# Attention's value bias added to the residual stream by GpSimd, row statistics gathered by fours, and the values of two batches by seven products of 129-column blocks

## The chip, the core and the metric

The kernel runs on one core of a Trainium2 chip. The core has a matrix engine (TensorE, PE in the profile; PEld are its weight loads), VectorE (DVE), ScalarE (ACT), GpSimd (POOL) and SyncE (SP, which here issues DMAs only). The metric is the device time of one execution in microseconds (us), as the median of several runs.

## The reference

The input x has 4 batches of 1024 tokens with 256 features, in fp32. Four blocks follow each other, each behind a layer normalization and with a residual:

```python
x = x + attention(layernorm(x))      # causal, one head of 256
x = x + ffn(layernorm(x))            # r * (relu(k)**2 @ Wv), token shift
x = x + state_space(layernorm(x))    # gated, with a long convolution
x = x + ffn(layernorm(x))            # same weights as before

# attention
Q, K, V = X @ Wq.T + bq, X @ Wk.T + bk, X @ Wv.T + bv
weights = softmax(where(causal, -inf, Q @ K.T / 16))
return weights @ V
```

A row of softmax weights sums to one, so `weights @ (X @ Wv.T + bv)` is `weights @ (X @ Wv.T) + bv`.

## The kernel before

**Tiles.** A batch is two halves of 512 tokens, numbered j (0 to 7), and a half is four row tiles of 128 tokens, numbered i over the whole input (0 to 31). The suffixes a, f, h, g of names stand for the four blocks: attention, first ffn, state space, second ffn. All matrix products are fp32, which TensorE does in two passes each; the profile counts the passes.

**Order.** The kernel first logs all its work with an `Order` object. `o.unit` logs a piece of TensorE work and `o.op` a piece of other work, with what it needs, and with one or several ways (an engine and an estimated cost). A planner then chooses the order and, for each op with several ways, the engine that would end first (`_way`, L256), and emits everything in that order. So the queue of each engine is fixed when the program is built, and each engine works its queue in order. Buffers in PSUM are two pairs of banks ("pair") and four single banks ("bank"). A pool of 34 slots of 4 x 257 numbers per partition holds what is as large as half a batch.

**Normalization** (`normalized`, L584). Per row tile VectorE makes `bn_stats` (st, L622) and `bn_aggr` (mv, L623). Then, for all four rows (in the first half, two and two), VectorE adds epsilon (ve, L648), GpSimd raises to the power -1/2 (rs, L661), VectorE makes the shift (mrs, L670), and VectorE (L676) or ScalarE (L682) makes each normalized row (xn). The rows are then turned to features by tokens, by transposes on TensorE (pt, L775 and L1455) or through DRAM.

**Attention.** Scores are taken as x M x^T with M made from both weights, so that only one side ("queries") is projected, and the other is the stream xa itself. `values(i)` (L1512) makes the values of a row tile: two products of 257 columns into a bank (pv, L1522), of which 256 are the value features and the last gives a score bias of the key side; VectorE then adds the bias row `bv_r` to all 257 and writes v (L1532). `scores(i)` (L1536) makes up to 1024 scores (sc, L1550), and VectorE adds the mask to the diagonal block (L1560) and takes the row's minimum with v's last column added (L1566); ScalarE makes the exponents (L1571). `weigh(i)` (L1647) multiplies with the values (po, L1655), and VectorE scales this and adds it to the stream x (L1664).

**Seven products** (`seven_products`, L840). A product of 2 x 2 blocks by seven block products instead of eight, used for the queries of batches 2 and 3 (`queries_of_batch`, from `SEVEN_FROM`), for the gates (zs), skips (ss) of the state block and for keys (gks) of the second ffn. It works on a chain in PSUM: p1, p6, p7, p4 follow each other in one bank, p5 and p3 in another, p2 in a third. Between them copies u1, u2, u3 (L783 on ScalarE, L784 on VectorE) and adds c11, c22, c12 (L905, L907) are made, and c21 is the end of the chain:

```python
unit(6, ..., [f"{key}.u1", f"{sums_key}.T2"], chain, first=False)
kept("u2", 6, 1)
...
unit(7, ..., [f"{key}.u2", f"{sums_key}.T3"], chain, first=False)
kept("u3", 7, 0, [f"{key}.c11"])
```

T1 to T4 are sums of blocks of the stream (`stream_sums`, L815: GpSimd or VectorE, L832); the sums of weight blocks are made once (`weight_sums`, L808).

**Second ffn.** `pr` (L928) are row products: pr_g.pr the gate, pr_g.pv the values, which need ka_g, the squared relu of the keys (ScalarE L1046 and L1047 for one of a chain's quarters). The stages after attention overlap with it and with each other; of the last half, g7, nothing follows but its own work.

Of the kernel before, what the change touches and what calls it, by code (L numbers as in the profile page):

```python
# [19 lines left out]
P = 128  # L20
NB = 4
L = 1024
D = 256
# [7 lines left out]
SLOT = 4 * (D + 1)  # L31
# [22 lines left out]
class Order:  # L54
# [17 lines left out]
    SURE = 0.5  # L72
    FRONT = 12.0
# [182 lines left out]
    def _way(self, time, n):  # L256

        if self.log[n]["moves"]:
            time = max(time, self.queue - self.FLIGHT - 0.5)
        return min(  # L260
            (self._start(time, w) + w[1], self._start(time, w), w[0], w[2])
            for w in self.log[n]["ways"]
        )
# [96 lines left out]
def dve(n):  # L360
    return 0.02 + n / 850
# [7 lines left out]
def hybrid_kernel(  # L369
# [41 lines left out]
    slots = ctx.enter_context(tc.tile_pool(name="slots", bufs=34))  # L411
# [92 lines left out]
    wv = new("wv", KC, D + 1)  # L504
    bv_r = new("bv_r", D + 1)
    bq_c, bk_c, dsk, dt_c = (new(n, KC) for n in ("bq_c", "bk_c", "dsk", "dt_c"))
# [14 lines left out]
    load(2.0, "wv", *stream_rows(wv[:, :, :D], WvT), *per_row(bv_r[:, :D], bv))  # L521
# [62 lines left out]
    def normalized(  # L584
# [36 lines left out]
        def stats(n):  # L621
            nc.vector.bn_stats(st()[:, n, :], row(n))  # L622
            nc.vector.bn_aggr(mv()[:, n, :], st()[:, n, :])  # L623
# [69 lines left out]
        if by_scalar:  # L693
            for n in range(NH):
                o.op(f"{key}.su{n}", [needs[n]], ("ACT", act(D) + 0.11, partial(sums, n)))
            o.op(f"{key}.me", [f"{key}.su{n}" for n in range(NH)], ("POOL", 0.2, means))
            for n in range(NH):
                o.op(f"{key}.st{n}", [f"{key}.me"], ("ACT", act(D) + 0.11, partial(squares, n)))
            variances_of = lambda n0, n1: by_sums()
            shifts_of = lambda n0, n1: shifts_by_sums()  # L700
        else:
            for n in range(NH):
                o.op(f"{key}.st{n}", [needs[n]], ("DVE", 0.53, partial(stats, n)))
            variances_of, shifts_of = variances, shifts
        for n0, n1 in spans:
            span = "" if n1 - n0 == NH else f"{n0}"
            some = range(n0, n1)
            o.op(
                f"{key}.ve{span}", [f"{key}.st{n}" for n in some],
                ("DVE+port", 0.08 * k, partial(variances_of, n0, n1)),  # L710
            )
            o.op(
                f"{key}.rs{span}", [f"{key}.ve{span}"],
                ("POOL", 0.4 + 0.62 * k, partial(powers, n0, n1)),
            )
            o.op(
                f"{key}.mrs{span}", [f"{key}.rs{span}"],
                ("DVE+port", 0.08 * k, partial(shifts_of, n0, n1)),
            )
            for n in some:  # L720
                o.op(
                    f"{key}.xn{n}", [f"{key}.mrs{span}"],
                    ("DVE+port", dve(D), partial(on_vector_by_sums if by_scalar else on_vector, n)),
                    ("ACT", act(D) + 0.1, partial(on_scalar, n)),
                )
# [89 lines left out]
    def stream_sums(key, src, needs):  # L815

        t = [lazy(lambda k=k: cols(f"T{k}_{key}")) for k in range(KC)]

        def b(c, h):
            return src(h)[:, c, :]  # L820

        def sums(k):
            return t[(k - 1) // 2]()[:, (k - 1) % 2, :]

        for k, plus, minus in (
            (1, lambda: b(0, 1), lambda: b(0, 0)),
            (3, lambda: b(1, 1), lambda: b(0, 1)),
            (2, lambda: b(1, 1), lambda: sums(1)),
            (4, lambda: b(1, 0), lambda: sums(2)),
        ):  # L830
            def emit(engine, k=k, plus=plus, minus=minus):
                engine.tensor_sub(sums(k), plus(), minus())  # L832

            o.op(
                f"{key}.T{k}", needs + ([f"{key}.T{k - 1}"] if k in (2, 4) else []),
                ("POOL", 1.05, partial(emit, nc.gpsimd)), ("DVE+port", dve(HALF), partial(emit, nc.vector)),
            )
        return sums

    def seven_products(key, sums_key, a, s_of, src, t_of, add_to, direct, needs, there):  # L840


        u = lazy(lambda: slot(f"u_{key}"))
        held = lazy(lambda: pair(f"held_{key}"))

        def part(k):
            return lambda: u()[:, ts(k, HALF)]

        def chain():
            return held()[:, :HALF]  # L850

        def shared():
            return held()[:, HALF:]

        def unit(r, w, data, need, dst, takes=None, first=True):
            o.unit(
                f"{key}.p{r}", columns(HALF), needs + need,
                lambda: nc.tensor.matmul(  # L858
                    dst(), lhsT=w(), rhs=data(), start=first, stop=True, skip_group_check=True
                ),  # L860
                takes,
            )

        def kept(name, r, k, more=()):
            o.op(f"{key}.{name}", [f"{key}.p{r}", *more], *copies(part(k), chain))

        unit(1, lambda: a(0, 0), lambda: src(0)[:, 0, :], there, chain, "pair")
        kept("u1", 1, 0)
        yield
        p = lazy(lambda: bank(f"p2_{key}"))  # L870
        unit(2, lambda: a(0, 1), lambda: src(0)[:, 1, :], there, p, "bank")
        o.op(
            f"{key}.c11", [f"{key}.p2", f"{key}.u1"],
            ("DVE", dve(HALF) + 0.03, partial(add_to, 0, 0, p, part(0))), frees="bank",
        )
        yield
        unit(6, lambda: s_of(2), lambda: t_of(2), [f"{key}.u1", f"{sums_key}.T2"], chain, first=False)
        kept("u2", 6, 1)
        yield
        unit(5, lambda: s_of(1), lambda: t_of(1), [f"{key}.p1", f"{sums_key}.T1"], shared)  # L880
        yield
        unit(7, lambda: s_of(3), lambda: t_of(3), [f"{key}.u2", f"{sums_key}.T3"], chain, first=False)
        kept("u3", 7, 0, [f"{key}.c11"])
        o.op(
            f"{key}.c22", [f"{key}.p5", f"{key}.u3"],
            ("DVE", dve(HALF) + 0.03, partial(add_to, 1, 1, shared, part(0))),
        )
        yield
        unit(4, lambda: a(1, 1), lambda: t_of(4), [f"{key}.u3", f"{sums_key}.T4"], chain, first=False)
        o.op(f"{key}.c21", [f"{key}.p4"], *direct(1, 0, chain))  # L890
        yield
        unit(
            3, lambda: s_of(4), lambda: src(1)[:, 1, :], [f"{key}.c22"] + there, shared, first=False
        )
        o.op(
            f"{key}.c12", [f"{key}.p3", f"{key}.u2"],
            ("DVE", dve(HALF) + 0.03, partial(add_to, 0, 1, shared, part(1))),
        )
        o.op(None, [f"{key}.c21", f"{key}.c12"], ("none", 0.0, lambda: None), frees="pair", lag=0.0)
        yield  # L900
# [45 lines left out]
    class Mix:  # L946
# [74 lines left out]
        def keys_of_batch(self, b):  # L1021
# [29 lines left out]
            for e, h in ((0, 0), (1, 1), (0, 1)):  # L1051
# [7 lines left out]
                key, key, fk_block, lambda k: fk_sums[:, k - 1, :], src, T,  # L1059
# [305 lines left out]
    def score_weights():  # L1365
# [42 lines left out]
        def store_behind():  # L1408
            nc.vector.tensor_scalar_mul(wv[:, :, D : D + 1], pm()[:, :, D : D + 1], -1.0 / 16.0)
# [27 lines left out]
    def attend_prepare(j, by_hand=False):  # L1437
# [6 lines left out]
        )  # L1444

# [44 lines left out]

    def queries_of_batch(b):
# [8 lines left out]
        T = stream_sums(key, src, there)  # L1500
        for name, needs in (
# [6 lines left out]
            key, key, wm_block, lambda k: q_sums[:, k - 1, :], src, T,  # L1508
# [3 lines left out]
    def values(i):  # L1512

        j, n = divmod(i, NH)
        if n == 0:
            v[j] = lazy(lambda: rows(f"v_{j}", D + 1))
# [3 lines left out]
        def emit():  # L1520
            for c in range(KC):
                nc.tensor.matmul(  # L1522
                    pv()[:, : D + 1], lhsT=xaj()[:, c, ts(n, P)], rhs=wv[:, c, :],
# [4 lines left out]
            f"pv{i}", columns(D + 1, 2), [f"a{j}.xa{c}" for c in range(KC)] + ["wvb"], emit, "bank"  # L1528
# [3 lines left out]
            ("DVE", dve(D), lambda: nc.vector.tensor_add(t()[:, n, :], pv()[:, : D + 1], bv_r)),  # L1532
            frees="bank",
        )

    def scores(i):  # L1536
# [21 lines left out]
        def least():  # L1558
# [3 lines left out]
            if i >= TURNED_BY_DRAM:  # L1562
# [4 lines left out]
                dst, src, v[2 * b + h]()[:, n, D : D + 1], None, ALU.add, ALU.min, accum_out=nmx(),  # L1567
# [15 lines left out]
        o.op(f"p{i}", [f"sc{i}", f"v{i}"], ("DVE", dve(nk) + 0.3, least), frees="pair")  # L1583
# [63 lines left out]
    def weigh(i):  # L1647
# [5 lines left out]
        def emit():  # L1653
            for n in range(t + 1):
# [3 lines left out]
                    rhs=v[2 * b + n // NH]()[:, n % NH, :D],  # L1658
# [15 lines left out]
        o.op(f"a.x{i}", [f"po{i}", f"rsm{i}"], ("DVE", dve(D) + 0.05, add), frees="bank")  # L1674
# [63 lines left out]
    def gates_of_batch(b):  # L1738
# [20 lines left out]
        for e, h in ((0, 0), (1, 1), (0, 1)):  # L1759
# [5 lines left out]
            key, key, wz_block, lambda k: z_sums[:, k - 1, :], src, T,  # L1765
# [162 lines left out]
    def skips_of_batch(b):  # L1928
# [3 lines left out]
        for j in (2 * b, 2 * b + 1):  # L1932
# [5 lines left out]
            f"ss{b}", f"zs{b}", wx_block, lambda k: x_sums[:, k - 1, :], src, sums_of_batch(b),  # L1938
# [3 lines left out]
    def mix_states(b):  # L1942
# [25 lines left out]
        for h in range(2):  # L1968
            j = 2 * b + h
            for e in range(KC):  # L1970
# [7 lines left out]
                    ("POOL", 1.05, partial(gated, nc.gpsimd, j, e)),  # L1978
# [74 lines left out]

    scored, valued = -1, 0
    for i in range(-2, NI):
# [18 lines left out]
        if 0 < j < 2 * NB:  # L2074
# [8 lines left out]
            if k == 3 and j % 2 == 1 and SEVEN_FROM <= j // 2 + 1 < NB:  # L2083
                chain = queries_of_batch(j // 2 + 1)
                behind = len(o.log)
        while valued < min(i + (3 if i < AHEAD_FROM else 4), NI - 1):
            valued += 1
            values(valued)
# [176 lines left out]
```

## Time and profile before

| | |
|---|---|
| median of three runs | 465.31 us (464.91 to 465.99) |
| the profiled execution | 464.18 us |
| its span in the profile | 462.4 us |
| TensorE, weight loads busy | 454.6, 311.4 us |
| VectorE, ScalarE, GpSimd busy | 370.7, 227.0, 139.4 us |
| granted TensorE clock | 1.00 |
| values: TensorE passes of 257 columns | 128 |
| values: VectorE adds | 32, 13.2 us |

The span is the time between the first and the last instruction that the profile shows. Busy times add up the instructions of an engine. A mean duration of a matmul is longer than its share of time, because matmuls are pipelined: how fast they follow each other is read from the starts of neighbours. "Idle before" and "waits" name the instruction whose end released an engine.

### The profile page before, as it was taken

Reading aid. Unit: us, or ns where it says so; the run is one execution under the profiler, and the core shown is the slowest. Engines: PE = TensorE matmul, PEld = TensorE weight load, DVE = VectorE, ACT = ScalarE, POOL = GpSimd, SP = SyncE. Lnnn points to the kernel's source line nnn. Section 1 sums busy time; section 2 is a strip of 40 time slices with the busy share of each in tenths; the row PEclk is TensorE's granted clock in tenths of the full one; section 3 lists DMA queues with packets and bytes.
Section 4 is the critical chain, followed back from the end, with each engine's and each line's share of the span. In section 5 each row is a group of like instructions: output and inputs, shape, how many; then the busy total and the mean of one; then the engine's idle time right before and its main releaser. Section 6 shows DMA issues by size and latency. Waiting matters only on the chain.

```text
span 462.4 us, 6630 instructions
## 1 busy us (share of the span) xinstructions
PE 454.6 (98%) x2052; PEld 311.4 (67%) x2052; DVE 370.7 (80%) x914; ACT 227.0 (49%) x473; POOL 139.4 (30%) x145
## 2 busy tenths in 40 slices
PE   8999999999999999999999999999999999999996
PEld 5665776667786767776678774473565857686675
DVE  4898697989989888788989977425689989998852
ACT  3322334453284453554335755523467887743452
POOL 3001002303032412332221568512255216336240
PEclk9999999999999999999999999999999999999999
DMA  8067958684358641428784869503014042604522
GB/s 236 27 170 209 272 143 236 169 252 151 101 160 213 184 138 51 137 87 256 226 261 128 276 220 276 213 15 90 13 63 121 0 143 86 215 14 135 178 75 68
DMA packets 84915, 69.44 MB, mean 150 GB/s; under 512 B 20160, under 2 KB 82576, under 8 KB 84880
## 3 DMA queue, kind: packets, MB, share of 16 engines
q1 hardware_dynamic: 84064, 68.76, 50.2%
q8 instruction: 16, 0.26, 0.2%
q10 hardware_dynamic: 816, 0.26, 0.2%
q14 instruction: 19, 0.16, 0.1%
HBM read 40.54 MB, written 28.45 MB: 149 GB/s over the span
## 4 chain that ended last, share of the span: by engine, by line
PE 84%; DVE 10%; POOL 3%; issue 1%; SPq 1%; DMA 1%; ACT 0%; DVEq 0%; POOLq 0%
PE po L1655 14%; PE sc L1550 13%; PE pv L1522 6%; PE held_zs L858 3%; PE held_ss L858 3%; PE held_qs L858 2%; PE held_gks L858 2%; PE pc L1862 2%; PE dust L1339 1%; DVE T_gks L832 1%; DVE xr_g L977 1%; DVE xk_g L977 1%; POOL x L1101 1%; PE pp_a0.pq L793 1%; PE pp_g6.pk L793 1%
## 5 line engine op out<-in xcount | busy, mean ns | idle before, releaser
L1655 PE MATMUL po<-v,prT 128*128 128x256 f32 x288 | 67.6, 380 | 0.0
L1550 PE MATMUL sc<-xa,q 128*128 128x512 f32 (+3 forms) x192 | 66.9, 486 | 0.0
L1655 PEld LDWEIGHTS po<-v,prT 128*128 128x128 f32 x288 | 54.2, 189 | 11.6 <-issue 3.1
L1571 ACT ACTIVATE pr<-pr,nmx 128x128 f32<-128x128 f32 (+7 forms) x32 | 24.7, 773 | 69.7 <-DVE pr L1566 57.1
L1550 PEld LDWEIGHTS sc<-xa,q 128*128 128x128 f32 x192 | 34.8, 190 | 24.3 <-issue 20.1
L1522 PE MATMUL pv<-wv,xa 128*128 128x257 f32 x128 | 32.7, 380 | 0.0
L1101 POOL TENSOR_TENSOR x<-x,r_f 128x512 f32<-128x512 f32 x16 | 20.8, 1298 | 35.7 <-DVE r_f L1095 33.8
L1522 PEld LDWEIGHTS pv<-wv,xa 128*128 128x128 f32 x128 | 23.9, 191 | 8.4 <-issue 4.1
L1608 DVE STREAM_TRANSPOSE prT<-pblocks 128x384 f32<-128x384 f32 (+7 forms) x30 | 24.0, 798 | 4.8 <-DMA pblocks<-exps 4.8
L661 POOL TENSOR_TENSOR rs_h<-ve_h,minus_half 128x8 f32<-128x8 f32 x8 | 13.2, 1646 | 47.9 <-DVE ve_h L650 47.9
L1566 DVE TENSOR_SCALAR_CACHE_REDUCE pr<-sc,v 128x128 f32<-128x128 f32 (+7 forms) x32 | 26.2, 818 | 1.1
L661 POOL TENSOR_TENSOR rs_a<-ve_a,minus_half 128x4 f32<-128x4 f32 x7 | 7.4, 1060 | 62.8 <-DVE ve_a L648 52.9
L1101 POOL TENSOR_TENSOR x<-x,r_g 128x512 f32<-128x512 f32 x14 | 20.1, 1446 | 16.8 <-DVE r_g L1095 16.8
L1699 POOL TENSOR_TENSOR x<-x,bout_r 128x512 f32<-128x512 f32 x16 | 20.7, 1302 | 13.3 <-ACT x L1692 9.8
L1692 ACT ACTIVATE x<-x,mrs_h,rs 128x256 f32<-128x256 f32 x32 | 17.2, 588 | 6.5 <-DVE rs L1703 6.5
L1965 POOL TENSOR_TENSOR z<-z,skip 128x512 f32<-128x512 f32 x11 | 15.0, 1384 | 17.4 <-DVE skip L1961 17.3
L661 POOL TENSOR_TENSOR rs_f<-ve_f,minus_half 128x4 f32<-128x4 f32 x8 | 8.1, 1016 | 39.2 <-DVE ve_f L648 34.1
L1664 DVE SCALAR_TENSOR_TENSOR x<-po,rsm,x 128x256 f32<-128x256 f32 x32 | 14.9, 467 | 5.4 <-PE po L1655 5.3
L622 DVE BATCH_NORM_STATS2 st_a<-x 128x6 f32<-128x256 f32 x32 | 13.0, 407 | 3.0 <-DMA x<-in_L_attn_a_X_dram 3.0
L974 ACT ACTIVATE xk_g<-hT_g,muk 128x512 f32<-128x512 f32 x16 | 11.0, 713 | 8.4 <-DVE hT_g L750 8.4
L1532 DVE TENSOR_TENSOR v<-pv,bv_r 128x257 f32<-128x257 f32 x32 | 13.2, 413 | 2.2 <-PE pv L1522 1.8
L977 DVE SCALAR_TENSOR_TENSOR xr_g<-hT_g,mur,xr_g 128x512 f32<-128x512 f32 x16 | 14.4, 920 | 0.5 <-ACT xr_g L974 0.5
(478 smaller groups left out, 1070.3 us busy)
## 6 DMA issues: line engine op xcount, KB each, us to landing
hk<-r_dram SPq DMA_DIRECT2D x16, 512.0 KB, 6.6
rows_g<-xn_g SPq DMA_DIRECT2D x8, 512.0 KB, 3.0
blocks_g<-rows_g SPq DMA_DIRECT2D x32, 128.0 KB, 2.7
x<-in_L_attn_a_X_dram SPq DMA_DIRECT2D x7, 512.0 KB, 5.1
rows_f<-xn_f SPq DMA_DIRECT2D x7, 512.0 KB, 3.5
blocks_f<-rows_f SPq DMA_DIRECT2D x28, 128.0 KB, 2.7
rows_h<-xn_h SPq DMA_DIRECT2D x7, 512.0 KB, 3.3
blocks_h<-rows_h SPq DMA_DIRECT2D x28, 128.0 KB, 2.9
```

Of the source, the lines that this page charges most:

```text
L661: nc.gpsimd.tensor_tensor(rs()[:, :k].rearrange("p k n -> p (k n)"), ve()[:, :k].rearrange("p k n -> p (k n)"), minus_half[:, : k * NH], A ...
L858: lambda: nc.tensor.matmul(dst(), lhsT=w(), rhs=data(), start=first, stop=True, skip_group_check=True),
L977: nc.vector.scalar_tensor_tensor(t()[:, c, :], hT()[:, c, :HALF], mu1[:, c : c + 1], t()[:, c, :], ALU.mult, ALU.add,)
L1101: nc.gpsimd.tensor_add(xg, xg, r()[:, ts(g, 2), :])
L1522: nc.tensor.matmul(pv()[:, : D + 1], lhsT=xaj()[:, c, ts(n, P)], rhs=wv[:, c, :], start=(c == 0), stop=(c == KC - 1),)
L1550: nc.tensor.matmul(sc()[:, k * HALF : k * HALF + w], lhsT=qh()[:, c, ts(n, P)], rhs=keys[k]()[:, c, :w], start=(c == 0), stop=(c == KC - 1),)
L1566: nc.vector.tensor_scalar(dst, src, v[2 * b + h]()[:, n, D : D + 1], None, ALU.add, ALU.min, accum_out=nmx(),)
L1571: nc.scalar.activation(p()[:, :nk], p()[:, :nk], AF.Exp, bias=nmx(), scale=-1.0, accum_out=sm())
L1608: nc.vector.transpose(dst()[:, : NH * width].rearrange("p (k m a) -> p k m a", m=NH, a=GRP), blocks().rearrange("p m (k a) -> p k m a", a= ...
L1655: nc.tensor.matmul(po()[:, :D], lhsT=src()[:, ts(n, P)], rhs=v[2 * b + n // NH]()[:, n % NH, :D], start=(n == 0), stop=(n == t),)
L1692: nc.scalar.activation(xt, xt, AF.Identity, bias=mrs()[:, 0, n : n + 1], scale=rs1()[:, n : n + 1])
L1699: nc.gpsimd.tensor_add(xg, xg, bout_r.unsqueeze(1).to_broadcast([P, 2, D]))
```

## The change

1. **Value bias.** `values` no longer adds `bv_r`. The values are copied out of PSUM by ScalarE or VectorE, and GpSimd adds the bias only in the last column (`whole_bias`, one [128 x 1] add per row tile, for which the minimum now waits). GpSimd adds bv to the stream x itself, once per two row tiles, after these rows have been normalized (`shifted`); the add of the attention's output to x waits for it.
2. **Statistics.** The four `bn_aggr` of a half are made together after its `bn_stats`.
3. **Layout.** The value weights get a zero column in front, so that they have 258 columns in two blocks of 129. The values stand in columns 1 to 256.
4. **Values by seven products** for batches 2 and 3, in two groups of row tiles per batch. Each product is two matmuls of 129 columns, one per row tile, with the sums T of the queries' chain as weights and blocks of the value weights (or their sums `v_sums`) as moving data. The chain takes two single banks. The queries' and the values' chains of a batch are logged alternately (`attended`).
5. **Planner.** VectorE gets a handicap of 0.5 us where another engine could do an op (`SPARED`); the estimated cost of two GpSimd ops goes from 1.05 to 1.25; there are 33 slots instead of 34, each a little larger.

```diff
-SLOT = 4 * (D + 1)
+VW = D + 2
+SLOT = 4 * VW
...
+    SPARED = 0.5
...
+        for engine, cost, emit in ways:
+            start = self._start(time, (engine, cost, emit))
+            late = start + cost
+            if len(ways) > 1 and engine[:3] == "DVE":
+                late += self.SPARED
+            if late < best:
+                best, chosen = late, (start + cost, start, engine, emit)
...
-    slots = ctx.enter_context(tc.tile_pool(name="slots", bufs=34))
+    slots = ctx.enter_context(tc.tile_pool(name="slots", bufs=33))
...
+    nc.gpsimd.memset(wv[:, :, 0:1], 0.0)
...
         def stats(n):
             nc.vector.bn_stats(st()[:, n, :], row(n))
-            nc.vector.bn_aggr(mv()[:, n, :], st()[:, n, :])
+
+        def gather(n0, n1):
+            for n in range(n0, n1):
+                nc.vector.bn_aggr(mv()[:, n, :], st()[:, n, :])
...
-                ("POOL", 1.05, partial(emit, nc.gpsimd)), ("DVE+port", dve(HALF), partial(emit, nc.vector)),
+                ("POOL", 1.25, partial(emit, nc.gpsimd)), ("DVE+port", dve(HALF), partial(emit, nc.vector)),
...
+    def row_products(tiles, width, *of):
+
+        def emit(dst, w, data, first):
+            for n, t in enumerate(tiles):
+                nc.tensor.matmul(
+                    dst()[:, ts(n, width)], lhsT=data()[:, ts(t, P)], rhs=w(),
+                    start=first and n == 0, stop=True, skip_group_check=True,
+                )
+
+        return len(tiles) * width, columns(width, len(tiles)), operands(*of), emit
...
+        def shifted(g):
...
+            nc.gpsimd.tensor_add(xg, xg, bv_r[:, :D].unsqueeze(1).to_broadcast([P, 2, D]))
+
+        for g in range(2):
+            o.op(
+                f"a{j}.b{g}", [f"a{j}.xn{2 * g + n}" for n in range(2)] + ["wv"],
+                ("POOL", 1.27, partial(shifted, g)), delay=1.0 + g,
+            )
...
         o.op(
             f"v{i}", [f"pv{i}"],
-            ("DVE", dve(D), lambda: nc.vector.tensor_add(t()[:, n, :], pv()[:, : D + 1], bv_r)),
-            frees="bank",
+            *copies(lambda: t()[:, n, :], lambda: pv()[:, :VW], VW), frees="bank",
         )
+        whole_bias(i)
...
+            ("POOL", 0.15, lambda: nc.gpsimd.tensor_add(
+                t()[:, n, D + 1 :], t()[:, n, D + 1 :], bv_r[:, D:])),
...
+    def values_of_batch(b, T):
...
+        for g in range(2):
+            key = f"vs{b}{g}"
...
+            yield from seven_products(
+                key, f"qs{b}",
+                row_products(
+                    range(2 * g, 2 * g + 2), VW // 2, wv_block, lambda k: v_sums[:, k - 1, :], src, T
+                ),
+                add_to, direct, ["v_sums"], there, kind="bank",
+            )
...
-        o.op(f"p{i}", [f"sc{i}", f"v{i}"], ("DVE", dve(nk) + 0.3, least), frees="pair")
+        o.op(f"p{i}", [f"sc{i}", f"vc{i}"], ("DVE", dve(nk) + 0.3, least), frees="pair")
...
+    def attended(b):
+
+        queries = queries_of_batch(b)
+        next(queries)
+        yield
+        values = values_of_batch(b, query_sums[b])
+        for _ in range(6):
+            next(queries)
+            yield
+            next(values)
+            yield
+        for _ in values:
+            yield
```

## The prediction

> **What bounds the kernel now.** I read the busy line and the slices first, then the stages, the waits of TensorE (PE), the chain, the groups. The page:
>
> ```profile
> PE 454.6 (98%) x2052; PEld 311.4 (67%) x2052; DVE 370.7 (80%) x914; ACT 227.0 (49%) x473; POOL 139.4 (30%) x145
> PE   8999999999999999999999999999999999999996
> DVE  4898697989989888788989977425689989998852
> PEclk9999999999999999999999999999999999999999
> ```
>
> PE is busy throughout at a full granted clock; VectorE (DVE) is second, 90% busy or more in many slices. A busy PE need not be at its pace, so the stages (span from start to end; PE, PEld, DVE, ACT, POOL busy) and PE's waits come next:
>
> ```profile
> 140.00:180.00 40.00, 40.00 (x161) 26.76 (x160) 34.49 (x85) 16.94 (x31) 12.74 (x16) 1.00 0.57 161
> 285.00:300.00 15.00, 14.71 (x70) 6.25 (x69) 7.23 (x15) 8.66 (x16) 8.41 (x8) 1.00 0.69 256
> 336.00:370.00 34.00, 34.00 (x133) 23.73 (x132) 30.97 (x51) 25.06 (x77) 14.85 (x18) 1.00 0.20 63
> 370.00:400.00 30.00, 30.00 (x113) 19.69 (x112) 27.41 (x52) 24.14 (x62) 13.03 (x12) 1.00 0.42 132
> ...
> PE pr_g4.pv L928 <- ACT ka_g L1047: 0.9, 1, 0.9
> PE held_gks L858 <- DVE u_gks L784: 0.9, 1, 0.9
> PE held_zs L858 <- DVE z L907: 0.6, 1, 0.6
> PE pt_h7.T L775 <- DVE xn_h L676: 0.3, 1, 0.3
> ```
>
> In attention (to about 285 us) PE never waits, though DVE is 86 to 90% busy: relieving DVE there buys nothing by itself. PE's waits after the start come to 2.7 us here, 3.3 us by start-to-start times. So the change can gain what it takes from PE's own work, plus some of those 3.3, less what it adds in waits.
>
> PE's pace is read from the chain (start, length, count of passes; an fp32 product is two passes):
>
> ```profile
> 18.38 0.87 PE pv L1522 x4
> 20.86 0.87 PE pt_a1.xa L1455 x8
> ```
>
> A value pass (257 columns) takes 0.87/4 = 0.217 us, a 128-column pass with its own weights 0.87/8 = 0.109. In the timeline two 512-column passes start at 407.63 and the next work at 408.49: 0.43 each. Time is proportional to columns from 512 to 128.
>
> **Part by part.** *Seven products, batches 2 and 3.* Out go 16 row tiles of 4 passes: 64 x 0.217 = 13.9 us. In come 4 groups x 7 products x 2 tiles x 2 passes = 112 passes of 129 columns, at 0.110: 12.3 us. The other 64 passes grow by one column, 0.05 in all. Net **-1.5 us**, all on the path.
>
> [...]
>
> *VectorE's relief.* The rows:
>
> ```profile
> L1532 DVE TENSOR_TENSOR v<-pv,bv_r 128x257 f32<-128x257 f32 x32 | 13.2, 413 | 2.2 <-PE pv L1522 1.8
> L1699 POOL TENSOR_TENSOR x<-x,bout_r 128x512 f32<-128x512 f32 x16 | 20.7, 1302 | 13.3 <-ACT x L1692 9.8
> L783 ACT COPY u_gks<-held_gks 128x512 f32<-128x512 f32 x6 | 3.5, 583 | 3.3 <-PE held_gks L858 3.3
> ```
>
> The order of the changed program gives the counts. DVE loses 32 value adds (-13.2), 27 normalized rows that go to ScalarE (ACT; at 0.41, those of f at 0.56: -12.7), 6 copies u (-4.1), 5 relu steps (-3), and gains 12 chain adds at some 0.42 (+5): 28 less. Gathering the bn_aggr takes little busy time away, but the pair bn_stats and bn_aggr has a pitch of 0.53 now and four bn_aggr can follow each other at about 0.1: some 0.06 a tile, so its queue is shorter by about 6 more. ACT gets 27 x 0.59 + 15 value copies and 16 chain copies at about 0.38 (a 128x256 copy of wq) + 6 x 0.583 + 5 x 0.62 and a few more: +37, to 57% of the span. POOL gets 16 bias adds at 1.30 (20.8), 32 one-column adds at 0.18 (its two-column copies: 5.8), and a net few stream sums: about +32. All of it lies beside PE work in attention: scores run two or three rows ahead of the minimum that now waits for the one-column add. Cost taken: nothing; if that cover failed, each late minimum would cost its POOL queue, about 1.3 us. The bias adds move no DMA; SP's queue keeps its order but for hk loads issued later with some 5 us in hand.
>
> When POOL reads SBUF, DVE pays: a T_gks sum took 1.64 us beside a POOL sum and 0.69 just before it; mrs_g took 1.23 beside an x add, 0.15 otherwise. [...]
>
> *The start.* Both later rows of the first normalization now go to ACT (before: DVE 9.65 to 10.06 and ACT 9.98 to 10.57), and both xa copies too (before one each, at 10.99 and 11.61). Two ACT rows in line end one 0.52 pitch later; a stall of 0.1 goes. **+0.45** (0.1 to 0.7).
>
> *The chains.* Each product of a chain waits for a copy of the last one: PE, then a copy of 0.38, then PE, about 0.65 us with the hand-overs, against units of 0.87 put between. One link looks short: in batch 2, second group, p4 waits for u3, which waits until DVE's c11 has read u1's place, and c11 stands behind the minimum of a long score row (0.82 on average, 1.2 for the longest). Its cover is one unit of 0.9. **+0.4** (0 to 1.5 for all 16 links).
>
> *The wait at 287* (pt_h7, 0.45 by start times). The new order puts the first products of the zs chain and one py product ahead of these transposes, and xn_h7 on ACT with about 1 us in hand: **-0.45** (0 to -0.7).
>
> *The wait at 424* (1.03 by start times). The chain there:
>
> ```profile
> 421.77 1.03 POOL rs_g L661
> 422.80 0.02 issue
> 422.82 1.23 DVE mrs_g L670
> 424.05 0.33 DVE xn_g L676
> 424.37 0.61 DVE u_gks L784
> ```
>
> u2 stands on DVE behind mrs_g6, and that behind eight pairs of statistics. I set the new order out by hand from the end of ka_g3's p3 (407.6 here), where p7 falls due after 16.4 us of PE work. [...]
>
> *Staying:* the wait at 430 (1.08: ACT's relu and square behind p3, same order) and at 324.6 (0.75: DVE's queue ahead of z is 6.6 against 6.5 us). *ACT's other copies:* all nine u_gks and u_ss on ACT now, in a stage where it is busy 49.2 of 64 us (336 to 400) and gets about 4 more. In the second gks chain u1 stands behind a relu and a row; p6 is due at 0.86 after p1, the copy ends at about 1.1: **+0.3** (0 to 2). The pool of slots, 33 for 34, lets the same reuses wait (pc_0): 0.
>
> Sum: -1.5 + 0.45 + 0.4 - 0.45 - 0.6 + 0.3 = **-1.4 us**. The profiled execution is 464.18 us (span 462.4), 1.1 below the median of the three runs; against it 462.8, against the median 465.31 - 1.4 = **463.9**.
>
> **Rivals.**
> - *Eaten up:* the chain links and ACT cost 1 to 1.5 us more than taken, or the wait at 424 stays. Speaks for it: each link has tenths in hand. -0.7 to +0.7: about 465.3.
> - *Slower, ACT the late one in 336 to 400:* it goes to 53 of 64 us and is in order; its worst ten microseconds (360 to 370) are at 9.8 busy already. It decides once u1 or u2 of a gks chain stands behind more than 0.3 us of rows waiting for a power on POOL; then each of about six links adds 0.3 to 0.5: +2 less nothing regained, 466.5 to 468. Against it: PE has no wait there now.
> - *More regained:* a lighter DVE also frees the waits at 324.6 and 424 wholly: another -1 to -2, about 462.2.
> - *The 129-column pass at its weight load's 0.19 us* (the PEld rows' mean) instead of 0.110: 112 x 0.08 = +9, about 473. The transposes with a load each at 0.109 speak against it.
>
> **Chances.** 0.2% is 0.93 us, about what a measurement of this kernel can tell from no change. The sum holds (-0.7 to -2.3) 0.50, of which 0.42 beyond -0.93; eaten up 0.17; ACT late 0.17; more regained 0.11; weight load 0.05. Faster 0.42 + 0.11 = 0.53; same 0.08 + 0.17 = 0.25; slower 0.22. The range from 462.4 to 466.8 leaves out the weight load, half of ACT late (0.09) and half of more regained (0.05): 0.19.
>
> **What would show it.** PE matmuls become 2100 (2052 - 64 + 112); value passes of two batches 0.110 apart; DVE near 343 us, ACT 264, POOL 171; the first queries about 0.45 later; no wait at pt_h7, a shorter one for p7 of the last gks chain, the two others unchanged. Wrong: new PE waits above 0.5 us in a vs chain or a gks chain, naming ACT u or DVE v.

## The result, and the profile after

The changed kernel takes 467.19 us (median of 22 executions, 465.20 to 468.44) against 464.96 for the kernel before (22 executions): a ratio of 1.0037, interval 1.0024 to 1.0050. It was forecast at 463.9, faster; it is slower, and above the range's end of 466.8.

The 22 executions fall into two groups by the granted TensorE clock of the whole span: ten at 0.998 to 1.000 with a median of 465.5 us, twelve at 0.994 to 0.996 with 467.6. The profiled one is of the second group. Its page, busy time and granted clock in 40 slices:

```profile
PE 454.9 (98%) x2100; PEld 313.5 (67%) x2100; DVE 342.1 (74%) x850; ACT 256.8 (55%) x549; POOL 169.7 (36%) x198
PEclk9899999999999999999999999999999999999999
```

The relief came as counted: 2100 passes, VectorE (DVE) at 342 us (343 said), GpSimd (POOL) at 170 (171), ScalarE (ACT) at 257 (264). But TensorE (PE) is no less busy, and the second slice shows a clock below full. PE's waits (engine and tile, released by; us, times, longest):

```profile
PE held_zs L874 <- DVE z L953: 1.7, 1, 1.7
PE dust L1385 <- DVE idle L454: 1.2, 1, 1.2
PE held_gks L874 <- DVE xk_g L1023: 1.1, 1, 1.1
PE held_qs L874 <- ACT q L960: 1.0, 2, 0.7
PE pr_g4.pv L974 <- ACT ka_g L1093: 0.9, 1, 0.9
PE pt_a0.xa L1511 <- ACT xn_a L694: 0.6, 2, 0.5
```

The waits at 287 and 424 us are gone. The one at 325 has grown, the one at 430 stays, and three are new: at the start, in the queries' chains, in a gks chain. The start, from the timeline of PE (start, length), in the kernel before and in the changed one:

```profile
10.29 0.88 PE L1455 MATMUL pt_a0.xa<-ident,xn_a 128*128 128x128 f32 x4
11.01 0.51 PE L1397 MATMUL pb_w<-bk_c,bq_w 128*128 128x1 f32 x4
11.63 3.70 PE L793 MATMUL pp_a0.pq<-xa,wq 128*128 128x512 f32 x8
...
9.84 0.47 PE L1435 MATMUL pb_w<-bq_c,wk_n 128*128 128x1 f32 x3
10.80 0.33 PE L1511 MATMUL pt_a0.xa<-ident,xn_a 128*128 128x128 f32 x1 [0.48 <-ACT xn_a L694]
11.29 0.55 PE L1511 MATMUL pt_a0.xa<-ident,xn_a 128*128 128x128 f32 x3 [0.16 <-ACT xn_a L694]
12.30 4.89 PE L812 MATMUL pp_a0.pq<-xa,wq 128*128 128x512 f32 x7
```

After the bias products PE has little to do until 12.30 (11.63 before). Then the stage from 12 to 16 us (its span; PE, PEld, DVE, ACT, POOL busy; the granted clock; DMA), again before and after:

```profile
12.00:16.00 4.00, 4.00 (x12) 2.08 (x11) 2.74 (x13) 1.32 (x3) 1.01 (x1) 1.00 0.10 32
...
12.00:16.00 4.00, 3.88 (x7) 1.79 (x7) 2.58 (x10) 0.79 (x3) 2.25 (x2) 0.57 0.05 16
```

The clock is 0.57 there on average; it was 1.00 in the kernel before. Four passes of the first queries start 0.72 to 1.01 us apart instead of 0.43, in all 1.6 us lost.

By start-to-start times the profiled execution adds up so, in us: passes of the values -1.3 (112 at a median of 0.112); first queries +0.67; clock +1.6; queries' chains +1.63 (0.84 at 115, 0.29 and 0.50 at 180 and 182); wait at 287 -0.58; wait at 325 +1.07 (1.82 for 0.75); gks chain at 393 +1.27; wait at 424 -1.03. Sum +3.3; the spans differ by 3.0 (465.4 and 462.4), and the other 0.3 is spread over smaller differences. The medians differ by less, 2.2, because the profiled execution of the kernel before, 464.18, is 0.8 below its median.

### The profile page after: what moved, and what is told of

It reads as the page before. It is cut to its first block, busy times and chain, and to the rows that moved or that the text cites. A ratio compares the mean times of both kernels' runs of the same rounds, so it can differ in the third digit from the quotient of the medians.

```text
span 465.4 us, 6831 instructions
## 1 busy us (share of the span) xinstructions
PE 454.9 (98%) x2100; PEld 313.5 (67%) x2100; DVE 342.1 (74%) x850; ACT 256.8 (55%) x549; POOL 169.7 (36%) x198
## 4 chain that ended last, share of the span: by engine, by line
PE 92%; DVE 4%; ACT 2%; SPq 1%; DMA 1%; issue 0%; DVEq 0%; ACTq 0%
PE po L1768 13%; PE sc L1663 13%; PE held_gks L874 3%; PE held_zs L874 3%; PE pv L1580 3%; PE held_ss L874 3%; PE held_qs L874 2%; PE held_vs L884 2%; PE pc L1975 2%; PE pp_a0.pq L812 1%; PE dust L1385 1%; PE pb L1912 1%; PE pp_g6.pk L812 1%; PE pr_f6.pr L974 1%; PE pr_f2.pv L974 1%; PE pr_f0.pv L974 1%
## 5 line engine op out<-in xcount | busy, mean ns | idle before, releaser
L1599 POOL TENSOR_TENSOR v<-v,bv_r 128x1 f32<-128x1 f32 x32 | 5.9, 198 | 56.0 <-ACT v L802 51.6
L1494 POOL TENSOR_TENSOR x<-x,bv_r 128x512 f32<-128x512 f32 x16 | 21.4, 1354 | 4.1 <-ACT xn_a L694 4.1
L2079 POOL TENSOR_TENSOR z<-z,skip 128x512 f32<-128x512 f32 x13 | 16.7, 1304 | 15.8 <-DVE skip L2075 15.8
L1673 DVE TENSOR_TENSOR sc<-sc,mask 128x128 f32<-128x128 f32 x32 | 9.5, 296 | 12.7 <-PE sc L1663 12.5
L1580 PE MATMUL pv<-wv,xa 128*128 128x258 f32 x64 | 16.2, 381 | 0.0
L694 ACT ACTIVATE xn_f<-x,mrs_f,rs_f 128x256 f32<-128x256 f32 x25 | 13.6, 591 | 3.7 <-DVE mrs_f L682 3.5
L1580 PEld LDWEIGHTS pv<-wv,xa 128*128 128x128 f32 x64 | 12.0, 191 | 4.4 <-issue 2.4
L694 ACT ACTIVATE xn_h<-x,mrs_h,rs_h 128x256 f32<-128x256 f32 x26 | 13.9, 590 | 1.9 <-DVE mrs_h L682 1.9
```

The costliest lines, as they stand in the source:

```text
L694: nc.scalar.activation(place(n), split(row(n)), AF.Identity, bias=mrs()[:, k - 1, n : n + 1], scale=rs()[:, k - 1, n : n + 1],)
L1494: nc.gpsimd.tensor_add(xg, xg, bv_r[:, :D].unsqueeze(1).to_broadcast([P, 2, D]))
L1580: nc.tensor.matmul(pv()[:, :VW], lhsT=xaj()[:, c, ts(n, P)], rhs=wv[:, c, :], start=(c == 0), stop=(c == KC - 1),)
```

## The experiments

Of the two kernels the order of all work, as their planner chose it, was recorded. Unless said otherwise an experiment emits such a recorded order with a few steps moved, so that nothing else changes; a planner's new order would change waits everywhere. A chain's pair is its buffer of two PSUM banks. Names of steps: a0.b0 is the bias add of the first two row tiles, a0.xn2 a normalized row, a0.xa1 a copy of transposed rows. Ratios are to the kernel before, run beside each experiment. "First queries" is their start in the one profiled execution; how early an execution gets under way moves it too (the first transposes stand at 8.68 to 9.69 us), so it is compared from these: 2.59 us before, 3.37 in the changed kernel.

**e1_start: the start put back**

```diff
-a0.xn2, a0.xa1 (ScalarE)
+a0.xn2, a0.xa1 (VectorE; with it the two small steps wvb)
-a0.b0 behind a0.xn2; a0.b1 behind a1.rs
+a0.b0, a0.b1 behind a1.xn3
```

> The changed kernel's recorded order of work, with the start alone put back: both bias adds of the first half come behind the second half's normalized rows on GpSimd, one late row xn_a0 and one copy xa go to VectorE as before. Theory (a late start lets the clock fall): TensorE's gap at 10 to 11.3 us closes, the first queries start near 11.65 instead of 12.30, every execution has the clock at 1.000, and the median comes to 464.5 to 465.2 instead of 467.2 (0.6 less than the 465.5 of the executions without the fall). Rival (the fall has nothing to do with the gap, for instance with the changed loads at the start): about half of the executions still show 0.994 to 0.996 and stand 2 us above the others.

465.76 us, ratio 1.0016 (1.0006 to 1.0025). All 11 executions have the clock at 0.998 to 1.000, the first queries start at 11.75, 2.59 behind the first transposes as before: the fall is tied to the start. The further 0.6 did not come: a new wait of 0.62 for a first score row at 19 us took it. GpSimd reached the moved bias adds early, at 14.8, mrs of the next rows took 1.22 beside them, and VectorE's queue was late with the minimum that frees the scores' buffer.

**e2_bias: only the bias adds moved**

```diff
-a0.b0 behind a0.xn2; a0.b1 behind a1.rs
+a0.b0, a0.b1 behind a1.xn3
```

> As e1_start, but only the two bias adds are moved; both late rows and both copies stay on ScalarE. [...] Rival (the rows on ScalarE make the gap): the queries start near 12.2 and the fall stays in half of the executions, 467.

467.21 us, ratio 1.0049 (1.0032 to 1.0065). mrs_a takes 0.15 again (0.64 in the changed kernel), and from the start of the bias products to the next transposes it is 1.14 us instead of 1.43 (0.81 before). But the first queries start as late as 12.39, 3.07 behind the first transposes, and seven of the eight executions show the fall (0.995 or 0.996). I had taken the bias add beside mrs_a for the main cause; it is 0.3 of the gap, the rows and copies on ScalarE are the rest, and enough for the fall.

**e3_dust: PE kept busy in the gap**

```diff
+keep_going(4)
 a0.pt0.2 (transposes of the late rows)
```

> The changed kernel's order with four more filling products (bf16, 512 columns) on TensorE just ahead of the late transposes of the first rows, where it idles; nothing else moves. Theory (the idle stretch lets the clock fall): no execution shows the fall, though the first queries start as late as in the changed kernel, 12.3; median 465.5, the time of its executions at full clock. Rival (the lateness itself, or the engines beside it): half of the executions at 467.5 as now.

465.72 us, ratio 1.0012 (1.0003 to 1.0021); all 11 executions at 0.998 to 1.000, with the first queries at 12.29, 3.16 behind the first transposes. The same stage:

```profile
12.00:16.00 4.00, 3.88 (x11) 1.89 (x11) 2.59 (x10) 1.41 (x3) 2.26 (x2) 1.00 0.07 24
```

At full clock, and late by 0.57 of the changed kernel's 0.78: it is PE's idleness before 12.3 us that lets the clock fall, not the engines beside it or the lateness.

**e4_before_late: the kernel before with that start**

```diff
-a0.xn2, a0.xa1 (VectorE)
+a0.xn2, a0.xa1 (ScalarE)
+x[0][:, 0:2, :] * 1.0 (GpSimd, behind a0.rs2)
```

> The kernel before, its order kept, with the changed kernel's late start alone: both late rows xn_a0 and both copies xa on ScalarE, and a GpSimd pass over two row tiles of x (times one, in place) where the bias add stands. Theory: the first queries start at about 12.2 to 12.3 instead of 11.63, and some of the executions, about half, show the clock at 0.994 to 0.996: these 2.0 + 0.6 us above before, the others 0.6; median 465.6 to 467.6. Rival (the fall comes from another part of the change): all executions at 1.000, median 465.6.

465.19 us, ratio 1.0009 (0.9994 to 1.0024). The first queries start at 12.45; four of 12 executions have the clock at 0.994 or 0.995, with a median of 466.9, the other eight 464.8. One of the four was profiled:

```profile
12.00:16.00 4.00, 3.88 (x8) 1.79 (x9) 2.33 (x11) 0.89 (x2) 1.04 (x1) 0.57 0.08 26
```

The late rows and copies on ScalarE bring the fall, without anything else of the change, in a third of the executions rather than half. The GpSimd pass did not play the bias add's part: mrs_a takes 0.15 in the midst of it (at 9.92; the pass, 1.51 long, starts at 8.88), and the start is that of e2_bias, 3.07 behind the first transposes. What I can't explain: the eight others are no slower than the kernel before, though the profiled one's queries come 0.48 later behind its first transposes.

How long the fall lasts can be read from the three profiles that have it, the changed kernel's, e2_bias's and e4_before_late's (the same columns as above):

```profile
12.19:15.60 3.41, 3.30 (x4) 1.51 (x5) 2.18 (x8) 0.54 (x2) 2.19 (x2) 0.50 0.03 11
13.06:16.48 3.42, 3.42 (x6) 1.36 (x5) 2.27 (x6) 0.69 (x1) 2.97 (x3) 0.50 0.00 0
12.49:15.90 3.41, 3.41 (x4) 1.47 (x5) 2.12 (x11) 0.40 (x1) 1.04 (x1) 0.50 0.00 0
```

In all three the clock is halved for 3.4 us. It falls 0.11 us ahead of the first queries, 0.67 behind their start and 0.04 behind it, so not at one step of the program.

**e5_links: the queries' chains**

With e3_dust's filling products, as the next three.

```diff
-qs2.c21 ahead of qs2.p3; qs3.c21 ahead of qs3.p3
+qs2.c21 behind qs2.p3; qs3.c21 behind qs3.p3
-vs31.p5 behind qs3.p4
+vs31.p5 ahead of qs3.p4
```

> The changed kernel's order with the four filling products of e3_dust (no fall of the clock), and with the queries' chains of batches 2 and 3 mended: the copy c21 is put behind p3 in the program instead of ahead of it, and one value product (vs31.p5) ahead of the queries' p4. Theory (the two halves of a chain's pair of banks count as one buffer, so that p3 waits for c21's read of the other half, which it doesn't need): TensorE's waits of 0.84, 0.29 and 0.50 us at 115, 180 and 182 go, 1.5 in all; 465.7 to 464.2. Rival (p3's own need, c22 on VectorE, is as late): the waits stay, named after VectorE, 465.7.

465.28 us, ratio 1.0014 (1.0005 to 1.0023). The three waits are gone, the one at 180 covered by the value product that was moved, the two others by the place of c21. So the theory of the pair holds: p3 needs only c22, but c21's read of the other bank had to end first, as the changed kernel's chain of waits at 115 us shows (c22, c21, p3):

```profile
114.34 0.76 DVE q L953
115.10 0.02 issue
115.13 0.70 ACT q L960
115.82 0.04 issue
115.87 1.13 PE held_qs L874 x2
```

The time does not follow: no gain by the ratio, 0.5 by the last matmul of the profiles (459.72 to 459.23). Waits of 0.39 and 0.32 for score rows (116 and 184 us) came in their place; the rest is not settled.

**e6_zs_gks: VectorE's order at 327 and 393 us**

```diff
-zs3.T2 ahead of zs2.c22
+zs3.T2 behind zs2.c22
-g2.xk0 behind g3.xk0
+g2.xk0 ahead of g3.xk1
-g3.xr1, gks1.T1, gks1.T3, gks1.T2, gks1.c11
+gks1.T1, gks1.T2, gks1.T3, gks1.c11, g3.xr1
```

> As e3_dust, with VectorE's order changed at two places: the stream sum T2 of the next gates' chain goes behind c22 of the chain before it (327 us), and xk_g2's first half goes ahead of xk_g3's, with the sums T1 and T2 ahead of xr_g3 (393 us). Theory (what the planner moved to VectorE and put in front there made the two waits): the waits of 1.82 and 1.27 go to 0.3 or less, 465.7 to 462.8 to 463.3. Rival (VectorE has too much to do there, whatever comes first): the next link waits instead, a gain of under 1 us.

463.66 us, ratio 0.9984 (0.9975 to 0.9993): 1.6 us below e5_links, run beside it, but above the 462.8 to 463.3 of the theory. At 325 us the wait falls from 1.82 to 0.15. In the changed kernel VectorE's timeline there was:

```profile
326.36 1.75 DVE L851 TENSOR_TENSOR T_zs<-xnT,T_zs 128x512 f32<-128x512 f32 x1
328.03 0.74 DVE L953 SCALAR_TENSOR_TENSOR z<-held_zs,b_all,u_zs 128x512 f32<-128x512 f32 x1
```

A sum that GpSimd made before, now on VectorE, ahead of c22, and 1.75 long (0.68 for the next such sum) beside a gate's product on GpSimd. At 393 it comes as the rival has it, though not by VectorE: the wait for xk_g goes, and the next link waits 1.10 instead, behind ScalarE's u1:

```profile
PE held_gks L974 <- ACT u_gks L902: 0.9, 1, 0.9
```

**e7_all: both** (edits of e5_links and e6_zs_gks)

> e5_links and e6_zs_gks together: all four new waits and the fall of the clock gone. By the theory that the loss lies in these places alone, the prediction's gain comes out: 465.7 - 1.5 - 2.7 = 461.5, some 3.5 below the kernel before. If waits move elsewhere, 462.5 to 464.

463.22 us, ratio 0.9971 (0.9959 to 0.9982): 0.3% faster than the kernel before, but not 461.5; the second branch came, in which waits move elsewhere. It is 0.4 below e6_zs_gks (0.5 from the first query to the last matmul), so that the queries' chains are worth 0.4 to 0.5, not 1.5.

**e8_plain_values: the change without seven products for values**, planned anew

```diff
-                chain = attended(j // 2 + 1)
+                chain = queries_of_batch(j // 2 + 1)
...
-            if valued < 2 * NH * SEVEN_FROM:
-                values(valued)
+            values(valued)
```

> The changed kernel without its seven products for values: batches 2 and 3 have their values made row tile by row tile, as batches 0 and 1; planned anew, with the four filling products at the start. Theory (seven products save 1.5 us of passes, but their chains, put between the queries' products, cost about as much in waits): TensorE has no waits at 115 and 180, its passes are 1.5 us longer; within 0.7 of e3_dust's 465.7. Rival (the seven products are a gain or a loss by themselves): over 1 us away, after the waits at 327 and 393, if they differ, are taken off.

468.48 us, ratio 1.0082 (1.0068 to 1.0096). As expected PE has no waits at 115 and 180. But planned anew, the last stage has its own: 1.6, 1.8, 0.8 and 1.0 us between 416 and 431, more than all that was to be measured. Two of its five executions are at 0.996 in spite of the filling products; its profile is at 1.000, so where the clock fell in the two is not shown. The experiment does not tell what the seven products are worth.

**e9_no_handicap: the change without VectorE's handicap**, planned anew, no filling products

```diff
-    SPARED = 0.5
+    SPARED = 0.0
```

> The changed kernel with VectorE's handicap of 0.5 us in the planner set to 0, planned anew, no filling products. Theory (the handicap is what moves the late rows and copies of the start to ScalarE): one late row and one copy stand on VectorE again, the clock falls in none or few of the executions; the rest is another order with waits of its own, 464 to 466.5. Rival (the bias add at the start alone is enough): the fall stays in half of the executions, 466 to 468.

468.61 us, ratio 1.0088 (1.0074 to 1.0102). One late row and one copy are on VectorE again, the first queries start at 11.62, and all four executions are at 0.999 or 1.000: the handicap had moved the rows. The time lies outside my 464 to 466.5: this order too has waits of its own in the last stages (1.6 at 430, 1.0 at 425, 0.9 at 292).

**e10_all_u1: e7_all, and u1 of the second gks chain earlier**

```diff
-g2.g1, g4.xn0, gks1.u1 (ScalarE)
+gks1.u1, g2.g1, g4.xn0
```

> As e7_all, and in the second gks chain ScalarE makes u1 first, ahead of a gate's sigmoid and a row that waits for a power. Theory (p5 waits for u1 there, 1.10 us at 391, only because u1 reads the other half of the same pair and stands late on ScalarE): the wait goes to about 0.25, what T1 needs, and 463.2 becomes 462.3. Rival (T1 and T2 on VectorE are as late): no change.

463.51 us, ratio 0.9977 (0.9967 to 0.9987); no gain over e7_all's 0.9971. The wait of 1.10 falls to 0.32, but 0.25 appears at the next gate, and the last matmul comes where it came (457.70 and 457.65, with the queries 0.25 later at the start, so 0.2 less from the first query). So u1's place did hold p5 up, against the rival, but of the 0.8 taken from that wait 0.2 reaches the end; where the rest goes is only partly shown.

**e11_before_mended: the kernel before, its own two waits mended**

```diff
-y0.1, zs2.c22 (VectorE)
+zs2.c22, y0.1
-gks2.u2 (VectorE, behind g6.xn0)
+gks2.u2 (ScalarE, ahead of g4.ka0)
```

> The kernel before with its recorded order mended at its own two waits: c22 of the zs chain goes ahead of a gate's product on VectorE (325 us), and u2 of the last gks chain to ScalarE (424 us). Theory (the waits are of the order, not of the arithmetic): 0.65 and 1.03 us go, 464.6 to 465.1 becomes 463.0 to 463.5; then the seven products and the relief are worth about 1 us between equally mended orders (e10_all_u1 below this). Rival: other links wait there instead, under 0.5 gained.

463.23 us, ratio 0.9973 (0.9958 to 0.9987): the 0.75 falls to 0.15, the 1.03 goes. So equally mended orders of the two kernels stand side by side, e10_all_u1 at 0.9977: from the first query to the last matmul it is 444.8 us against 445.0. The 1.5 us of passes are hardly to be seen. Interleaved with other work the 112 passes take 12.9 us (0.115 each), which leaves 1.1. Of the other 0.9 some 0.6 are waits: those above 0.12 us come to 2.5 us in e10_all_u1 and 1.9 here; the rest is open.

**e12_best: e10_all_u1 with a good start instead of filling products**

```diff
-keep_going(4)
-a0.xn2, a0.xa1 (ScalarE)
+a0.xn2, a0.xa1 (VectorE, with wvb)
-a0.b0 behind a0.xn2; a0.b1 behind a1.rs
+a0.b0 behind vc1; a0.b1 behind a2.rs
+p0 ahead of a2.st2; p1 ahead of a2.st0
```

> As e10_all_u1, but without the filling products: the start as in the kernel before (one late row and one copy xa on VectorE), GpSimd's bias adds of the first half put behind the small adds of the first value rows, where VectorE's blocked instructions hold nobody, and the first minima a little earlier on VectorE. Theory (the late start is what still holds e10_all_u1 back): the first queries start near 11.8 instead of 12.4 and nothing waits at 19 us, 463.5 to 462.8, and the clock stays up. Rival (VectorE's queue hands the lateness on to the scores of the first rows, as in e1_start): 463.5.

462.93 us, ratio 0.9957 (0.9943 to 0.9970), the lowest of all; all five executions at full clock, the first queries 2.59 behind the first transposes, no wait at 19 us. From the first query to the last matmul it is 444.9 us, as in e10_all_u1 and e11_before_mended, so that by the profiles its gain over e10_all_u1 lies in the start. Its waits of PE, the two longest:

```profile
PE dust L1485 <- DVE idle L554: 1.2, 1, 1.2
PE pr_g4.pv L1074 <- ACT ka_g L1193: 0.9, 1, 0.9
```

These two the kernel before has as well. Of the change there remain waits of 0.25 to 0.39 in the queries' chains and the second gks chain, 1.3 in all.

## Why the prediction was wrong

- *The passes* (-1.5): right in kind, a little large. The 129-column passes follow each other in 0.112 (-1.3), 0.115 on average among other work (-1.1), not at the weight load's 0.19.
- *The start* (+0.45): the step that failed most. The lateness itself was 0.67, within its 0.1 to 0.7, but it had a consequence that the step put at nothing and no rival priced: in 12 of 22 executions the clock falls for the first queries, which puts these 2.1 us above the others and the median above the range; the ten others, at 465.5, lie inside it. Shown by e1 (start back: no fall), e3 (gap filled: no fall) and e4 (the late rows and copies alone, in the kernel before: a fall). The filling products in front of it in the code were the hint that I passed over: I read the clock row as full and took it for given. The profile of before could not show how near it was to falling. In the three profiles that have the fall the clock is at half for 3.41, 3.42 and 3.41 us, and in the changed kernel's four passes of the queries start 0.72 to 1.01 us apart instead of 0.43. What sets that length, how idle TensorE must be for the fall, and in which executions it comes, no run here shows: e4_before_late and e2_bias have the same waits of TensorE at the start (0.20 and 0.16), and 4 of 12 and 7 of 8 executions fall.
- *The bias add at the start*: the bias add was costed at nothing, "beside PE work in attention". At the start there is no such cover: mrs_a, on the path, took 0.64 instead of 0.15, 0.3 of the gap by e2. What GpSimd's work beside it costs VectorE, which the trace of before showed in two places (1.64 for 0.69, 1.23 for 0.15), came due here and again at 327 us, where the sum T2 took 1.75 (0.68 for the next such sum). mrs_a ends at 10.11, just behind the bias add at 10.09. Beside the GpSimd pass of e4_before_late, which has one input, mrs_a took 0.15.
- *The chains* (+0.4, 0 to 1.5): 1.63 by the waits, and not by the mechanism I named (u3 behind c11 in the second group of batch 2, which did not wait). The values' products put between p4 and p3 gave c21 time to be emitted ahead of p3, and the chain's two banks count as one buffer. Yet mending it (e5, e7) gave back only some 0.5.
- *The wait at 324.6* ("staying", so at nothing): +1.07. I compared VectorE's queue by alone-standing durations, 6.6 against 6.5 us, and missed that T2 would meet GpSimd's product. Shown by e6.
- *ACT's other copies* (+0.3): the wait in the second gks chain was 1.27, but for xk_g on VectorE, put last of three. Here the place was right and the cause not the one that ended last: with xk_g moved ahead (e6), p5 waits 1.10 there for u1, the copy I had named for p6.
- *The waits at 287 and 424* (-0.45 and -0.6): both gone, -0.58 and -1.03. No run shows the -0.6; the changed kernel showed the wait of 1.03 gone whole. *The one at 430*: right, 1.08 in both.
- *The rivals*: "ACT the late one" had a price near the result's, but not its place. No chain waited for ScalarE by more than 1.1 us, and the stage from 336 to 400 us gave only one wait.

At full clock the changed kernel is 0.5 us slower than before where 1.4 less was forecast: the new waits are larger than what was gained. The rest of the 2.2 is the clock. That the gain sought is small beside what an order holds by chance is shown from three sides: e8 and e9, planned anew, are over 1 us slower than the changed kernel, e9 with no fall of the clock; e11, the old arithmetic with two steps moved, is as fast as the new arithmetic mended.

## What to carry to other kernels

A delay of PE's first real work can have a second price. Here it was 2.1 us of clock in 12 of 22 executions, and with four filling products in the gap the clock fell in none of 11: look at how empty the microseconds before that work are, and fill the gap before counting anything else. Where a planner orders everything anew, a change's own arithmetic of 1 or 2 us is lost among waits that the new order makes: record the order, mend it by hand, and compare mended with mended. And a buffer of two banks tracked as one makes a reader of one bank hold up the writer of the other (by 0.84 us at 115 here), as soon as the two stand in that order in the program.

## What was not expected of the hardware

- Waits of TensorE of 0.48 and 0.16 us within 2 us (starts 0.74 and 0.49 us apart, where such passes otherwise follow each other in 0.11), with only transposes and one-column products between, came with a fall of the clock in 12 of 22 executions; in the profiled one it is half for 3.41 us. With waits of 0.20 and 0.16 it fell in 7 of 8 (e2_bias) and 4 of 12 (e4_before_late).
- Four filling products of 0.22 us each in that gap kept it up in all 11 executions, and in all 36 of e5_links, e6_zs_gks, e7_all and e10_all_u1; in e8_plain_values, planned anew, two of five show a fall somewhere.
- VectorE's sum T2 took 1.75 us beside GpSimd's product, the next such sum alone 0.68; its small shift mrs 0.64 and 1.22, 0.15 alone, and 0.15 beside e4_before_late's GpSimd pass with one input.
